# Scale before square: reordering the two readers of the heads' values, and the fourth head's transposes, in a fused GNN/FFN kernel

## The chip, the cores and the metric

The kernel runs on one core of a Trainium2 chip. The metric is the device time of one execution in microseconds (us). The core has a matmul engine (PE), a vector engine (DVE), a scalar engine (ACT), a GpSimd engine (POOL) and a sync engine (SP) that issues most transfers. Each works through its own list of instructions in order, and they meet through semaphores.

## What is computed

The reference is two layers on 625 nodes of 512 features: a hyperbolic graph convolution, a mixture of experts, a second graph convolution, and a grouped-query attention with a two-step output map. All the work around the change is in that last block. Cut to what matters, it is

```python
q  = (xn @ Wq_w + Wq_b)                    # 128 heads of 128
qk = einsum('bsghd,blgd->bghsl', q, kc) / sqrt(128)
z  = einsum('bghsl,blgd->bsghd', softmax(qk), vc)   # 625 x (128 heads * 128)
zn = z / max(norm(z), 1e-12) * sqrt(16384) * wz_g1
h1 = silu(zn @ wz_w1 + wz_b1)              # 625 x 1024
```

So of each head's values z two things are needed: z times the gain wz_g1, which goes into the product with wz_w1, and z squared, whose sum over all heads gives the norm that scales the product afterwards.

## The kernel before, in words

The 128 heads are taken in 32 blocks of HB = 4. The loop at lines 1239 to 1263 is a software pipeline over the blocks: in step i it starts the loads of block i+1 (`load`), runs the product of block i-2 with wz_w1 (`hidden`, line 1209: 98 small products, a fast matrix multiplication on quarters of the operands), transposes the attention of block i-1 for its heads 0 and 1 (`transposes`, line 1144), folds the query weights of block i into keys (`folded`, line 1103), turns the query weights of block i+1 on DVE (`turned`, lines 1097 to 1101), computes the values of the four heads of block i-1 (`value`, line 1155), builds the operand sums of block i-1 for its product (`prepared`, line 1195), and computes the scores of block i with their softmax (`scores`, line 1114).

Per head h the work around the change is this.

- `transposes(b, h)`: five PE transposes of the attention into a PSUM tile `atps` (line 1150) and two ACT copies into the SBUF tile `attT[h % 2]` (line 1153). There are two attT tiles, so heads 0 and 2 share one and heads 1 and 3 the other.
- `value(b, h)`: two products into a PSUM tile `zps` (line 1159), the square on ACT into `zs` (line 1162), the scaling on DVE into `zT` (line 1163), and the addition of `zs` into the running sum `zsq`, on POOL (line 1166) but for the last block, where it is on DVE (line 1168). The tile zs has one buffer (`bufs=1`, line 1161).

After the last block, `combined` (line 1266) is ordered behind the last addition to zsq (`combined(inner(0), valued)`, line 1281), and the norm is made from zsq in `scale_of_values` (line 1296).

What sets the order: the code's order is only a priority. The framework takes the program as a graph of instructions and lays down one list for each engine by a timed plan of its own; an instruction that stands earlier in the code but whose inputs are not there yet in that plan can be passed by a later one. The plan also hands out buffers (the PSUM pool of this part has four slots of two banks, shared by atps, zps, kbps, scps and h1ps) and puts the semaphore waits in. Two engines that read the same PSUM tile are kept apart, in the order of the code: in the kernel before, DVE's scaling waits for ACT's square of the same zps.

In the texts below v0 to v3 are the value products of heads 0 to 3 of a block, t2 and t3 the PE transposes of heads 2 and 3, copy 2 and copy 3 their ACT copies, and square 0, scaling 0, addition 0 and so on the three steps of line 1162, 1163 and 1166.

Of the kernel before, what the change touches and what calls it, by code (L numbers as in the profile page):

```python
# [22 lines left out]
OP = mybir.AluOpType  # L23
# [16 lines left out]
QN = 157  # L40
# [15 lines left out]
HB = 4  # L56
# [111 lines left out]
def layers_kernel(  # L168
# [10 lines left out]
    nc = tc.nc  # L179
    V, A, T = nc.vector, nc.scalar, nc.tensor  # L180
# [22 lines left out]
    b1T, bqT, g1T, gmT, bkT, bz1T, g2T = (cols[:, a:b] for a, b in (  # L203
        (0, 128), (128, 256), (256, 384), (384, 388), (388, 396), (396, 404), (404, 412)))
# [43 lines left out]
    def moments(behind=None, pieces=((0, NT),)):  # L248

        st = rpool.tile([P, NT, V.BN_STATS_DIM], F32, tag="ln_st", name="ln_st")  # L250
        mv = rpool.tile([P, NT, V.BN_AGGR_DIM], F32, tag="ln_mv", name="ln_mv")
        rs = R.new("ln_rs")
        for a, b in pieces:
            for t in range(a, b):
                read = V.bn_stats(st[:, t, :], x[:, t, :])
                if behind is not None:
                    order(read, behind)
                V.bn_aggr(mv[:, t, :], st[:, t, :])
            V.tensor_scalar(rs[:, a:b], mv[:, a:b, 1], LN_EPS, None, op0=OP.add)
            R.act(rs[:, a:b], rs[:, a:b], AF.Sqrt)  # L260
            R.inverse(rs[:, a:b], rs[:, a:b])
        return mv, rs, read
# [50 lines left out]
    with ExitStack() as es:  # L313
# [138 lines left out]
        def rotating(name):  # L452
            return big.tile([128, NT * D], F32, tag="rotating", name=name, bufs=2)
# [86 lines left out]
        def conv_out(raw, mapped, last):  # L540

            acc = [psum.tile([128, 512], F32, tag="ps", name="agps") for _ in range(NT)]
            if last:
                busy(acc[0], 18, mapped)
            for a, b in PIECES:
                for t in range(NT):
                    for i in range(a, b):
                        product = T.matmul(acc[t][:P], AT[:, i, tp(t)], raw[:, i, :], start=i == 0, stop=i == NT - 1)  # L548
            u = None if last else rotating("u")[:P].rearrange("p (t n) -> p t n", n=D)
            sq, s, inside = (RP[0, NT].new(name) for name in ("co_sq", "co_s", "co_in"))  # L550
            for a, b in PIECES:
                r = RP[a, b]
                for t in range(a, b):
                    junk = work.tile([P, D], F32, tag="junk", name="junk")
                    A.activation(junk, acc[t][:P], AF.Square, scale=dis[:, t : t + 1], accum_out=sq[:, t : t + 1])
                    if not last:
                        V.tensor_scalar(u[:, t, :], acc[t][:P], dis[:, t : t + 1], None, op0=OP.mult)
                s_p, in_p = r.expmap0(sq[:, a:b], "co")
                if last:
                    R.mul(s[:, a:b], s_p, dis[:, a:b])  # L560
                    for t in range(a, b):
                        V.scalar_tensor_tensor(x[:, t, :], acc[t][:P], s[:, t : t + 1], x[:, t, :],
                                               op0=OP.mult, op1=OP.add)
                else:
                    V.tensor_copy(s[:, a:b], s_p)
                    V.tensor_copy(inside[:, a:b], in_p)
            if last:
                product = busy(psum.tile([128, 512], F32, tag="ps", name="spare"), 31, product)
            return u, s, inside, product
# [6 lines left out]
        u = rotating("u")[:P].rearrange("p (t n) -> p t n", n=D)  # L576
# [13 lines left out]
        b_scale, _ = R2.in_ball(*b_norm, "b")  # L590
        s, inside = r.in_ball(*norm, "ex")
# [15 lines left out]
        for first in range(GROUP, EC, GROUP):  # L607
            last = min(first + GROUP, EC)
            group = counting(first, last)
            for j in range(first, last):  # L610
# [3 lines left out]
                if j == first + 8 and first == GROUP:  # L614
                    ps = psum.tile([128, 512], F32, tag="ps", name="colps")
# [4 lines left out]
                    ps = psum.tile([128, 512], F32, tag="ps", name="gtps")  # L620
# [8 lines left out]
        u, s, inside, _ = conv_out(sent, mapped, False)  # L629
# [3 lines left out]
    with ExitStack() as es:  # L633
# [42 lines left out]
        for a, b in PIECES:  # L676
            ps = psum.tile([128, 512], F32, tag="ps", name="lps")
# [40 lines left out]
        for g in range(G):  # L718
            ps = psum.tile([128, 512], F32, tag="ps", name="wkps")
# [17 lines left out]
        ps = psum.tile([128, 512], F32, tag="ps", name="bbps")  # L737
# [93 lines left out]
        def second_map(e):  # L831
            oe = work.tile([CAP, D], F32, tag="oe", name="oe")
            ps = psum.tile([128, 512], F32, tag="ps", name="ops")
            for hc in range(HC):
                T.matmul(ps[:CAP], hT[e][:, hc, :], w2[e][:, hc, :], start=hc == 0, stop=hc == HC - 1)  # L835
            return oe, V.tensor_tensor(oe, ps[:CAP], b2[e], op=OP.add)
# [34 lines left out]
        for e in range(NE):  # L871
# [4 lines left out]
            if e + 1 < NE:  # L876
                chosen(e + 1)
                oe, _ = second_map(e)
# [5 lines left out]
        for t in range(NT):  # L884
            ps = psum.tile([128, 512], F32, tag="ps", name="yps")
# [14 lines left out]
    with ExitStack() as es:  # L900
# [8 lines left out]
        for k in range(2):  # L909

            sT = big.tile([128, DC, N], F32, tag="sT", name="sT", bufs=2)
            for c in range(DC):
                for a, b in PIECES:
                    ps = psum.tile([128, 512], F32, tag="ps", name="stps")
# [7 lines left out]
            for t in range(NT):  # L922
                ps = psum.tile([128, 512], F32, tag="ps", name="l1ps")
# [16 lines left out]
    with ExitStack() as es:  # L940
# [11 lines left out]
        mv, rs, _ = moments()  # L952
# [14 lines left out]
        for a, b in PIECES:  # L967
            ps = psum.tile([128, 512], F32, tag="ps", name="hps")
# [4 lines left out]
        for a, b in PIECES:  # L973
            ps = psum.tile([128, 512], F32, tag="ps", name="wtps")
# [4 lines left out]
        ps = psum.tile([128, 512], F32, tag="ps", name="wsps")  # L979
# [18 lines left out]
        ps = psum.tile([128, 512], F32, tag="ps", name="wsps2")  # L998
# [7 lines left out]
        ps = psum.tile([128, 512], F32, tag="ps", name="xmps")  # L1006
# [6 lines left out]
        ps = psum.tile([128, 512], F32, tag="ps", name="swps")  # L1013
# [8 lines left out]
        for q in range(2):  # L1022
            ps = psum.tile([128, 512], F32, tag="ps", name="kcps")
# [5 lines left out]
            for i in range(4):  # L1029
                g = 4 * q + i  # L1030
                V.scalar_tensor_tensor(kcT[:, g, :], sums[:, :L], bkT[:, g : g + 1], ps[:, i * L : (i + 1) * L],
                                       op0=OP.mult, op1=OP.add)
        for q in range(2):
            ps = psum.tile([128, 512], F32, tag="ps", name="vcps")
# [8 lines left out]
        for q in range(2):  # L1043
            ps = psum.tile([128, 512], F32, tag="ps", name="qbps")
# [9 lines left out]
    with ExitStack() as es:  # L1054
# [5 lines left out]
        zsq = big.tile([128, 4 * QN], F32, name="zsq")  # L1060
# [4 lines left out]
        zT = big.tile([128, 7, 2, 2 * QN], F32, name="zT")  # L1065
# [5 lines left out]
        NB = G * H // HB  # L1071
# [6 lines left out]
        def banks(name):  # L1078
            return psum.tile([128, 2, 512], F32, tag="ps", name=name)
# [64 lines left out]
        def transposes(b, h):  # L1144
            ps = banks("atps")
            if b == h == 0:
                busy(ps[:, 0], 13, folded.last)
            for k, (p0, p1) in enumerate(PIECES):
                for t in range(p0, p1):
                    T.transpose(ps[:L, k, (t - p0) * P : (t - p0 + 1) * P], att[b][:, t, h * L : (h + 1) * L],  # L1150
                                ident[:P, :P])
            for k, (p0, p1) in enumerate(PIECES):
                A.activation(attT[h % 2][:, p0 * P : p1 * P], ps[:L, k, : (p1 - p0) * P], AF.Copy)  # L1153

        def value(b, h):
            g = b * HB // H
            ps = banks("zps")
            for u in range(2):
                T.matmul(ps[:, u, : 2 * QN], vc[:, g * DH : (g + 1) * DH], attT[h % 2][:, 2 * u * QN : 2 * (u + 1) * QN],  # L1159
                         start=True, stop=True)  # L1160
            zs = work.tile([128, 2, 2 * QN], F32, tag="zs", name="zs", bufs=1)
            A.activation(zs, ps[:, :, : 2 * QN], AF.Square)  # L1162
            scaled = V.tensor_scalar(zT[:, h % 2 : 4 : 2, h // 2, :], ps[:, :, : 2 * QN], g1T[:, b * HB + h : b * HB + h + 1],  # L1163
                                     None, op0=OP.mult)
            if b < NB - 1:
                nc.gpsimd.tensor_tensor(zsq, zsq, zs.rearrange("p u s -> p (u s)"), op=OP.add)  # L1166
                return scaled
            return V.tensor_tensor(zsq, zsq, zs.rearrange("p u s -> p (u s)"), op=OP.add)

        def zsums(z, to):  # L1170

# [67 lines left out]
        for i in range(NB + 1):  # L1239
            if i + 1 < NB:  # L1240
                load(i + 1)
            if i >= 2:
                hidden(i - 2)
            if i >= 2:

                transposes(i - 1, 0)
                transposes(i - 1, 1)
            if i < NB:
                folded(i)
            if i == 1:  # L1250
                transposes(0, 0)
                transposes(0, 1)
            if i + 1 < NB:
                turned(i + 1)
            if i >= 1:
                for h in range(HB):
                    valued = value(i - 1, h)
                    if h + 2 < HB:
                        transposes(i - 1, h + 2)
            if 1 <= i < NB:  # L1260
                prepared(i - 1)
            if i < NB:
                scores(i)
# [150 lines left out]
```

## Time and profile before

| what | value |
| --- | --- |
| median of 3 runs | 2293.77 us (2293.68 to 2294.13) |
| the profiled execution's own time | 2299.3 us |
| its span, first to last instruction | 2297.5 us |
| PE busy | 2230.4 us (97%) |
| DVE busy | 1618.5 us (70%) |
| POOL busy | 991.4 us (43%) |
| ACT busy | 814.8 us (35%) |
| mean granted PE clock | 0.989 |
| first square of heads' values (L1162) | at 630.5 us |
| last scaling of heads' values (L1163) | at 2195.3 us |

The profiled execution took 5.5 us more than the median run, 0.24%. The four-head blocks run from about 627 us to 2197 us, more than two thirds of the span, and they are nearly alike: where one block is shown, it stands for the others. A row of the timeline gives the start in us from the span's start, the length in us, the engine, the line, the operation, the tile written and those read, the number of instructions merged in the row, and in brackets how long the engine sat idle before it and on whom it waited. A row of the waits gives who waited on whom: us in total, times, the longest in us. A busy PE says little of itself, since the matmuls overlap and their ends are modelled; the distance from one row's start to the next is the better measure.

### The profile page before, as it was taken

The numbers are of one execution on the slowest core, as the hardware profiler recorded it, in microseconds if no ns is written. First come the engines' busy times: TensorE is split into PE (matmuls) and PEld (weight loads), VectorE is DVE, ScalarE is ACT, GpSimd is POOL, SyncE is SP. The second block draws the span as 40 slices with busy tenths as digits, with TensorE's granted clock in tenths as the row PEclk, the third lists the DMA queues.
The fourth block names the chain that finished last, engine by engine and source line by source line (L and its number), as shares of the span: only waits on it lengthen the run. The fifth ranks groups of instructions, "written<-read, shape, count | busy, mean of one in ns | idle before, by whom it ended". The sixth has DMA issues, their size and how long they took to land.

```text
span 2297.5 us, 34432 instructions
## 1 busy us (share of the span) xinstructions
PE 2230.4 (97%) x12812; PEld 1770.4 (77%) x12812; DVE 1618.5 (70%) x2303; ACT 814.8 (35%) x2773; POOL 991.4 (43%) x1063
## 2 busy tenths in 40 slices
PE   8999999999999999999999999999999999999987
PEld 5746777756788888888888888888888888888853
DVE  5845333233478888877888887788888778888782
ACT  2354111111333443344344334433443443344322
POOL 1000000100265566656556665555666555566531
PEclk8999999999999999999999999999999999999989
DMA  7002688771222222233222223322222332221110
GB/s 256 8 0 87 233 295 297 237 238 40 36 65 60 59 66 59 60 96 73 59 59 66 59 60 96 73 59 59 66 59 59 96 72 61 59 66 41 42 59 23
DMA packets 326025, 204.68 MB, mean 89 GB/s; under 512 B 275534, under 2 KB 279563, under 8 KB 321000
## 3 DMA queue, kind: packets, MB, share of 16 engines
q1 hardware_dynamic: 317371, 189.65, 28.0%
q10 hardware_dynamic: 3639, 7.56, 0.9%
q0 software_dynamic: 4848, 5.26, 0.9%
q8 instruction: 102, 1.67, 0.3%
q14 instruction: 65, 0.53, 0.1%
HBM read 197.18 MB, written 5.23 MB: 88 GB/s over the span
## 4 chain that ended last, share of the span: by engine, by line
PE 86%; DVE 4%; ACT 4%; POOL 2%; issue 2%; DMA 1%; ACTq 0%; POOLq 0%; DVEq 0%
PE h1ps L1222 35%; PE scps L1123 19%; PE kbps L1110 5%; PE hps L824 5%; PE ops L835 5%; PE zps L1159 3%; POOL zsq L1166 2%; ACT zs L1162 2%; PE stps L918 2%; PE eps L77 2%; PE agps L548 2%; PE atps L1150 2%; PE l1ps L925 1%; DMA b_row<-in_L_gnn_b_dram 1%; DVE hacc L1270 1%
## 5 line engine op out<-in xcount | busy, mean ns | idle before, releaser
L1234 DVE TENSOR_TENSOR hacc<-hacc,h1ps 128x942 f32<-128x942 f32 (+1 forms) x510 | 529.2, 1084 | 11.6 <-PE h1ps L1222 11.6
L1123 PE MATMUL scps<-keys,xnT 128*125 128x400 f32 x1280 | 435.1, 499 | 0.0
L1182 POOL TENSOR_TENSOR wq<-wz 128x256 f32<-128x256 f32 x248 | 241.0, 981 | 405.5 <-PE h1ps L1222 347.3
L1123 PEld LDWEIGHTS scps<-keys,xnT 128*125 128x125 f32 x1280 | 240.0, 188 | 185.1 <-issue 2.6
L1131 ACT ACTIVATE att<-att,a_top 125x100 f32<-125x100 f32 x640 | 231.9, 364 | 361.6 <-DVE a_top L1126 361.6
L1222 PE MATMUL h1ps<-zT,wq 128*128 128x157 f32 x1736 | 302.6, 296 | 0.0
L1222 PE MATMUL h1ps<-zq,wq 128*128 128x157 f32 x1736 | 302.5, 297 | 0.0
L1166 POOL TENSOR_TENSOR zsq<-zsq,zs 128x628 f32<-128x628 f32 x124 | 187.6, 1513 | 201.6 <-ACT zs L1162 201.6
L1222 PEld LDWEIGHTS h1ps<-zT,wq 128*128 128x128 f32 x1736 | 256.2, 189 | 0.0
L1222 PEld LDWEIGHTS h1ps<-zq,wq 128*128 128x128 f32 x1736 | 255.9, 190 | 0.0
L1153 ACT ACTIVATE attT<-atps 100x375 f32<-100x375 f32 (+1 forms) x256 | 92.4, 432 | 397.3 <-PE atps L1150 397.3
L1182 POOL TENSOR_TENSOR wq<-wz,wq 128x256 f32<-128x256 f32 x248 | 210.8, 850 | 19.5
L1163 DVE TENSOR_SCALAR zT<-zps,cols 128x628 f32<-128x628 f32 x128 | 111.6, 872 | 149.0 <-ACT zs L1162 147.6
L1142 ACT ACTIVATE att<-att,a_tot 125x100 f32<-125x100 f32 x620 | 170.2, 365 | 10.7 <-DVE a_tot L1132 10.7
L1159 PE MATMUL zps<-attT,vc 100*128 100x314 f32 x512 | 160.9, 436 | 10.6 <-ACT attT L1153 10.5
L1182 POOL TENSOR_TENSOR wq<-wsum,wq 128x256 f32<-128x256 f32 x186 | 161.5, 868 | 14.7 <-POOL wq L1182 0.3
L1182 POOL TENSOR_TENSOR wq<-wsum 128x256 f32<-128x256 f32 x186 | 135.8, 730 | 65.0 <-PE h1ps L1222 65.0
L1222 PE MATMUL h1ps<-zT,wz 128*128 128x157 f32 x992 | 152.6, 296 | 0.0
L1101 DVE STREAM_TRANSPOSE wqT<-wqraw 128x512 f32<-128x512 f32 x128 | 80.3, 681 | 101.1 <-PE kbps L1110 84.2
L1222 PEld LDWEIGHTS h1ps<-zT,wz 128*128 128x128 f32 x992 | 141.0, 189 | 9.1
L1162 ACT ACTIVATE zs<-zps 128x628 f32<-128x628 f32 x128 | 88.7, 693 | 125.0 <-POOL zsq L1166 111.3
L1159 PEld LDWEIGHTS zps<-attT,vc 100*128 100x128 f32 x512 | 87.4, 191 | 45.9 <-ACT attT L1153 26.9
(408 smaller groups left out, 3438.3 us busy)
## 6 DMA issues: line engine op xcount, KB each, us to landing
w<-in_L_ffn_w_dram SPq DMA_DIRECT2D x16, 4096.0 KB
wz<-in_L_ffn_wz_w_dram SPq DMA_DIRECT2D x32, 2048.0 KB
wqraw<-in_L_ffn_Wq_w_dram SPq DMA_DIRECT2D x512, 64.0 KB
cb<-qbias SPq DMA_DIRECT2D x32, 195.3 KB
wkv<-in_L_ffn_Wkv_w_dram SPq DMA_DIRECT2D x1, 4096.0 KB
W_raw<-in_L_gnn_W_dram SPq DMA_DIRECT2D x2, 1024.0 KB
w<-in_L_ffn_Wkv_w_dram SPq DMA_DIRECT2D x1, 2048.0 KB
l1w<-in_L_gnn_W_dram SPq DMA_DIRECT2D x2, 1024.0 KB
```

The costliest lines, as they stand in the source:

```text
L824: T.matmul(ps[:, i * CAP : (i + 1) * CAP], w1[e][:, c, hc * 128 : (hc + 1) * 128], xgT[e][:, c, :], start=c == 0, stop=c == DC - 1)
L835: T.matmul(ps[:CAP], hT[e][:, hc, :], w2[e][:, hc, :], start=hc == 0, stop=hc == HC - 1)
L1110: folded.last = T.matmul(ps[:, k, h * L : (h + 1) * L], wqT[b][h][:, (c + k) * 128 : (c + k + 1) * 128], kcT[:, b * HB // H, :], start=Tru ...
L1123: T.matmul(ps[:P, t - t0, : HB * L], xnT[:, c, tp(t)], keys[b][:, c, :], start=c == 0, stop=c == DC - 1)
L1131: A.activation(own, own, AF.Exp, bias=top[:, t, h : h + 1], accum_out=tot[:, t, h : h + 1])
L1142: A.activation(own, own, AF.Copy, scale=tot[:, t, h : h + 1])
L1159: T.matmul(ps[:, u, : 2 * QN], vc[:, g * DH : (g + 1) * DH], attT[h % 2][:, 2 * u * QN : 2 * (u + 1) * QN], start=True, stop=True)
L1162: A.activation(zs, ps[:, :, : 2 * QN], AF.Square)
L1166: nc.gpsimd.tensor_tensor(zsq, zsq, zs.rearrange("p u s -> p (u s)"), op=OP.add)
L1182: engine.tensor_tensor(to, x, y, op=OP.subtract)
L1222: T.matmul(ps[:, at % 6 // 3, at % 3 * QN : (at % 3 + 1) * QN], now[j][:, m * 128 : (m + 1) * 128], zquarter[b][j][:, place[i]], start=Tru ...
L1234: V.tensor_tensor(to, to, got, op=OP.add)
```

## The change

`value` is cut in two. What stays in it are the products and DVE's scaling, which now stands first among the readers of zps; ACT's square and the addition to zsq move into a new function `squared`, called afterwards. With that, the order of the two readers of zps turns over: ACT's square comes behind DVE's scaling. In the loop the transposes of head 2 stay behind the square of head 0, and the transposes of head 3, which stood behind the square of head 1, now stand ahead of it (and behind the scaling of head 1). The last block takes the same path, its additions on DVE as before. What `valued` means at the end is the same, the last addition to zsq.

```diff
@@ value @@
             for u in range(2):
                 T.matmul(ps[:, u, : 2 * QN], vc[:, g * DH : (g + 1) * DH], attT[h % 2][:, 2 * u * QN : 2 * (u + 1) * QN],
                          start=True, stop=True)
+            return ps, V.tensor_scalar(zT[:, h % 2 : 4 : 2, h // 2, :], ps[:, :, : 2 * QN],
+                                       g1T[:, b * HB + h : b * HB + h + 1], None, op0=OP.mult)
+
+        def squared(b, ps):
+
             zs = work.tile([128, 2, 2 * QN], F32, tag="zs", name="zs", bufs=1)
             A.activation(zs, ps[:, :, : 2 * QN], AF.Square)
-            scaled = V.tensor_scalar(zT[:, h % 2 : 4 : 2, h // 2, :], ps[:, :, : 2 * QN], g1T[:, b * HB + h : b * HB + h + 1],
-                                     None, op0=OP.mult)
-            if b < NB - 1:
-                nc.gpsimd.tensor_tensor(zsq, zsq, zs.rearrange("p u s -> p (u s)"), op=OP.add)
-                return scaled
-            return V.tensor_tensor(zsq, zsq, zs.rearrange("p u s -> p (u s)"), op=OP.add)
+            engine = nc.gpsimd if b < NB - 1 else V
+            return engine.tensor_tensor(zsq, zsq, zs.rearrange("p u s -> p (u s)"), op=OP.add)
@@ the loop over blocks @@
             if i >= 1:
                 for h in range(HB):
-                    valued = value(i - 1, h)
-                    if h + 2 < HB:
-                        transposes(i - 1, h + 2)
+                    ps, _ = value(i - 1, h)
+
+                    if h == 1:
+                        transposes(i - 1, 3)
+                    valued = squared(i - 1, ps)
+                    if h == 0:
+                        transposes(i - 1, 2)
```

No instruction is added or taken away, and no transfer is touched.

## The prediction, made before the result was known

> **What bounds the kernel now.** I read the page first: PE is busy 97% of the span, and the chain that ended last is 86% PE. So an edit on DVE, ACT and POOL can only matter where PE waits for them. I then took the waits of PE within the blocks, one block's timeline, and the last block's. PE's rows of one block, from the products of the values to the scores:
>
> ```profile
> 1083.69 1.23 PE L1159 MATMUL zps<-attT,vc 100*128 100x314 f32 x4
> 1084.76 0.70 PE L1150 MATMUL atps<-ident,att 125*100 125x125 f32 x5
> 1085.29 1.23 PE L1159 MATMUL zps<-attT,vc 100*128 100x314 f32 x4
> 1086.86 1.33 PE L1159 MATMUL zps<-attT,vc 100*128 100x314 f32 x4 [0.34 <-ACT attT L1153]
> 1088.02 13.60 PE L1123 MATMUL scps<-keys,xnT 128*125 128x400 f32 x40
> ```
>
> These are v1, t3, v2, v3 and the first scores. From start to start, v1 takes 1.07 us (1083.69 to 1084.76), v2 1.57 and v3 1.16. Free-running, v2 and v3 would take 1.07 each. The hole before v3 is thus 0.50 + 0.09 = 0.59 us (the page shows 0.34 of it idle, since matmul ends are modelled). It is PE's only one in the block: from 1088.18 to 1128.52 PE is busy throughout. The same wait stands in the list of waits 31 times, once for each block but the last.
>
> Why v3 is late, by ACT's rows of the same stretch:
>
> ```profile
> 1083.42 0.69 ACT L1162 ACTIVATE zs<-zps 128x628 f32<-128x628 f32 x1 [0.31 <-PE zps L1159]
> 1084.01 0.74 ACT L1153 ACTIVATE attT<-atps 100x375 f32<-100x375 f32 x2
> 1085.74 0.69 ACT L1162 ACTIVATE zs<-zps 128x628 f32<-128x628 f32 x1 [0.99 <-POOL zsq L1166]
> 1086.33 0.75 ACT L1153 ACTIVATE attT<-atps 100x375 f32<-100x375 f32 x2
> ```
>
> Square 1 waits for POOL's addition 0 to give zs back (1084.19, 1.52 us long), and copy 3, whose transposes had started at 1084.76, is queued behind it. v3 starts 0.53 us after copy 3 does.
>
> DVE's rows, same block:
>
> ```profile
> 1081.60 2.49 DVE L1101 STREAM_TRANSPOSE wqT<-wqraw 128x512 f32<-128x512 f32 x4 [2.85 <-PE kbps L1110]
> 1084.14 0.87 DVE L1163 TENSOR_SCALAR zT<-zps,cols 128x628 f32<-128x628 f32 x1
> 1086.47 0.87 DVE L1163 TENSOR_SCALAR zT<-zps,cols 128x628 f32<-128x628 f32 x1 [1.45 <-ACT zs L1162]
> ...
> 1092.00 1.32 DVE L1173 TENSOR_TENSOR zT<-zT 128x628 f32<-128x628 f32 x1
> 1093.36 0.81 DVE L1174 TENSOR_TENSOR zT<-zT 128x628 f32<-128x628 f32 x1
> ```
>
> Each scaling starts 0.04 us after its square ends, so the two readers of zps are kept apart. And the four weight transposes hold DVE until 1084.09, well after v0 could be read (1083.42).
>
> **The change, part by part, in that block's times.**
>
> *Scaling ahead of square.* Scaling 0 can't start before the weight transposes end: 1084.14 as now, to 1085.01. Square 0 becomes the waiting one: 1085.05 instead of 1083.42, 1.63 us later. Behind it on ACT are queued copies 2 and 3, and behind those v2 and v3; its addition on POOL comes later too. Everything depends on whether copy 2 is held up.
>
> *Copy 2.* In the code it stays behind square 0. But the lists are laid down by what is ready: in the last block ACT runs, against the code,
>
> ```profile
> 2189.07 0.48 ACT L1153 ACTIVATE attT<-atps 100x375 f32<-100x375 f32 x1 [0.80 <-PE atps L1150]
> 2189.45 0.69 ACT L1162 ACTIVATE zs<-zps 128x628 f32<-128x628 f32 x1
> 2190.02 0.38 ACT L1153 ACTIVATE attT<-atps 100x250 f32<-100x250 f32 x1
> ```
>
> the first part of copy 3 ahead of square 1, because zs wasn't free yet. DVE likewise passes L1175 by L1176, which does not need the operand just made. Here copy 2's inputs come from t2, which starts at 1083.16 right behind v0 and lasts some 0.5 us, while square 0 needs scaling 0, over a microsecond later. I take copy 2 ahead of square 0: about 1083.7 to 1084.5, so v2 starts at 1085.29 as now, cost nothing. If the plan keeps the code's order, see the first rival.
>
> *Copy 3.* Its two ACT instructions and five PE transposes move ahead of square 1 and no transfer goes with them; on PE the order v1, t3, v2, v3 is unchanged, on POOL nothing is passed but addition 1, which isn't needed by PE, and SP sees nothing. Copy 3 now follows square 0 instead of square 1. A copy starts 0.59 us after its square (1083.42 to 1084.01): 1085.05 + 0.59 = 1085.64. v3 can start 0.53 later, 1086.17, and is due behind v2 at 1085.29 + 1.07 = 1086.36. It fits by 0.19 us, so the hole closes: scores at 1086.36 + 1.07 = 1087.43 instead of 1088.02, **0.59 us a block, 18.3 us over 31**. The bounds of this term: nothing, if copy 3 slips by 0.8, and 0.59, since PE has no other hole here.
>
> *What is late next.* Squares 1 to 3 now wait for the additions. Square 0 ends at 1085.74, addition 0 at about 1087.3, square 1 runs 1087.4 to 1088.1, square 2 ends at 1090.4, square 3 at 1092.7. They give back PSUM slots: the second scores tile (due 1087.43 + 2.7 = 1090.1, eight products at 0.336) needs the slot of v1, the third (1092.8) that of v2, the product after them (1100.9) that of v3. The margins are 2.0, 2.4 and 8.2 us, so this costs nothing. POOL's next work now starts at 1103.84, 11.18 us after its additions.
>
> *DVE's sums beside POOL's additions.* Scalings 1 to 3 no longer wait for squares; the last ends near 1088.6 (v3 at 1086.36, readable 1.35 later as v0 is, plus 0.87) instead of 1091.97. So the eight sums of `prepared` start 3.4 us earlier, but three of the additions now lie beside them. The row: L1173 takes 1.32 us beside addition 3, L1174 of the same size 0.81 alone, so 0.5 each, 1.5 us in all. The Trainium skill ("SBUF — State Buffer", section "SBUF: two separate sides") speaks harder against the change: a GpSimd instruction and a VectorE instruction with two SBUF inputs lock their common port pair for a whole instruction, and the loser fully blocks. The trace agrees as far as it goes: L1173 began 0.65 us before the addition ended (1091.14 + 1.51) and finished 0.67 us after. By start-to-start times the sums need 4 x 0.73 + 4 x 1.21 and one added scores row 0.90, 8.7 us: done at 1097.3 without contention, 1098.8 by the row, and 1101.3 by the rule with about 4.0 us of additions served in full. PE reads the last sum at 1102.52 now, at 1101.93 afterwards. So it is covered even by the rule, by 0.6 us. I take nothing.
>
> *Last block.* DVE makes the additions here. Now each head costs the chain square (0.70), scaling (0.87), addition (0.73 to 1.00): from square 1 at 2189.45 to the last addition at 2196.89. Afterwards a scaling can run while ACT squares the head before. Scaling 0 from 2186.9 (no weight transposes here), square 0 to 2188.7 with copy 2 ahead of it, scaling 1, addition 0 to 2190.1, and then per head a square (0.75) and an addition (0.8) with the scalings in the gaps: the last addition at about 2194.9. `combined` hangs on it and everything behind on DVE. **2.0 us**; between 0.3 (if every addition is queued ahead of the next scaling) and 3.5 (DVE's own 4 x 0.87 + 4 x 0.75 without a gap).
>
> The sum is 18.3 + 2.0 = 20.3 us. Against the profiled execution: 2299.3 to 2279.0. Against the median, which is 0.24% below that execution: 2293.77 - 20.3 = **2273.5**.
>
> **The rivals.**
>
> *Square 0 stays ahead of copy 2 on ACT (slower).* For it: the code says so. Against: the last block's rows. Then copy 2 starts at 1085.64, v2 at 1086.17 instead of 1085.29, with its first weight load exposed (+0.09) v3 follows at 1087.33, scores at 1088.40: 0.38 later than now, 11.8 us over 31 blocks, less 2.0: 2303.6. It decides from the point where v2 is more than 0.5 us late, that is when scaling 0 ends after about 1084.6; it ends at 1085.01.
>
> *The hole closes by half.* The 0.19 us that copy 3 has to spare goes, or sums blocked by additions come up to 0.3 us too late for PE. For it: both margins are thin. 0.3 x 31 = 9.3 us saved: 2284.5.
>
> *PE gains nothing in the blocks.* Copy 3 still ends behind a zs wait, or what PE gains it waits out at the product. Against: L1222 shows no idle PE at all, and POOL waits for PE there (L1182, 0.70 us a time), not the reverse. Only the last block gains: 2291.8.
>
> **How the numbers follow.** A measurement of this kernel can tell about 0.2% (4.6 us) from no change. Chances: forecast 0.70, half 0.14, nothing 0.07, slower 0.09. Faster by over 0.2% is 0.70 + 0.14 = 0.84, the same 0.07, slower 0.09. The low end is the hole closed and the last block's best: 18.3 + 3.5 = 21.8, with a little for the hole's own error: 2270. The high end takes in the half: 2286. That leaves out 0.16.
>
> **What would show it.** In the profile after: no wait of PE's L1159 on ACT L1153 in the blocks, scores starting 2.14 us after v2, a block period of 49.7 us instead of 50.3; on ACT copy 2, square 0, copy 3, square 1 in that order; L1162 waiting for DVE L1163, no longer the reverse; the sums L1173 to L1176 longer but ending before PE asks; the last L1168 some 2 us sooner after the last block's transposes. The prediction is wrong if square 0 stands ahead of copy 2, if PE's L1222 shows a wait for DVE, or if v3 still waits.

## The result, and the profile after

| | before | changed |
| --- | --- | --- |
| median | 2293.95 us (4 runs, 2293.68 to 2295.53) | 2312.22 us (4 runs, 2310.83 to 2316.06) |
| ratio, 95% interval | | 1.0073 (1.0061 to 1.0085) |
| profiled execution, span | 2299.3, 2297.5 us | 2310.83, 2309.1 us |
| from the first v0 to the last block's v0 | 1556.4 us | 1574.9 us |
| from the last block's v0 to the end | 112.0 us | 109.9 us |
| period of a block | 50.32 us | 51.00 us |
| DVE busy | 1618.5 us | 1715.5 us |

The kernel became slower by 0.73%, where 0.89% faster was forecast. The profiled executions differ by 11.5 us only, because the code ahead of the first values, which the change does not touch, happened to take 4.9 us less in the later one. The loss is in the blocks: 18.5 us; from the last block's values on, 2.1 us come back. The period of a block is the time from its v0 to the next block's v0.

First the forecast's own place. PE's timeline of a block of the changed kernel (scaling is now L1161, the square L1167, POOL's addition L1169, DVE's operand sums for the product L1174 to L1177, and L1235 the additions to hacc, DVE's running sum of the product in SBUF, each of which empties a PSUM slot):

```profile
1083.59 1.23 PE L1159 MATMUL zps<-attT,vc 100*128 100x314 f32 x4
1084.65 0.70 PE L1150 MATMUL atps<-ident,att 125*100 125x125 f32 x5
1085.19 2.29 PE L1159 MATMUL zps<-attT,vc 100*128 100x314 f32 x8
1087.31 13.60 PE L1123 MATMUL scps<-keys,xnT 128*125 128x400 f32 x40
...
1110.77 0.77 PE L1223 MATMUL h1ps<-zT,wq 128*128 128x157 f32 x4 [0.26 <-DVE hacc L1235]
...
1128.28 0.74 PE L1150 MATMUL atps<-ident,att 125*100 125x125 f32 x5 [0.20 <-DVE hacc L1235]
1129.33 1.92 PE L1110 MATMUL kbps<-kcT,wqT 128*128 128x100 f32 x15 [0.31 <-DVE hacc L1235]
```

v2 and v3 now run in one piece; from v2 to the scores it is 2.12 us, 2.73 before. The hole is closed. But there are three new ones, all waits for DVE's additions to hacc: PE needs a PSUM slot that DVE has not emptied. By starts they are 1110.77 instead of 1110.34, 1128.28 instead of 1127.91 and 1129.33 instead of 1128.81: 0.43 + 0.37 + 0.52 = 1.32 us. The block gained 0.61 and lost 1.3. The list of waits has each of the three 29 times: the first and the last of the 31 periods (49.77 and 46.19 us, before 50.40 and 46.79) gained 0.6 and lost nothing.

Why DVE is late, by its own timeline in the same block:

```profile
1088.42 1.69 DVE L1174 TENSOR_TENSOR zT<-zT 128x628 f32<-128x628 f32 x1
1090.14 0.81 DVE L1175 TENSOR_TENSOR zT<-zT 128x628 f32<-128x628 f32 x1
1090.88 2.12 DVE L1177 TENSOR_TENSOR zT<-zT 128x628 f32<-128x628 f32 x1
...
1093.76 2.50 DVE L1174 TENSOR_TENSOR zq<-zT 128x1099 f32<-128x1099 f32 x1
...
1099.93 0.99 DVE L1124 TENSOR_TENSOR att<-scps,cb 125x800 f32<-125x800 f32 x1
...
1104.86 2.17 DVE L1235 TENSOR_TENSOR hacc<-hacc,h1ps 128x942 f32<-128x942 f32 x2
1109.35 0.28 DVE L1132 RECIPROCAL a_tot<-a_tot 125x20 f32<-125x20 f32 x1 [2.32 <-ACT att L1131]
1109.55 6.30 DVE L1235 TENSOR_TENSOR hacc<-hacc,h1ps 128x942 f32<-128x942 f32 x6
```

and POOL's:

```profile
1090.25 2.08 POOL L1169 TENSOR_TENSOR zsq<-zsq,zs 128x628 f32<-128x628 f32 x1 [0.81 <-ACT zs L1167]
1093.13 1.96 POOL L1169 TENSOR_TENSOR zsq<-zsq,zs 128x628 f32<-128x628 f32 x1 [0.81 <-ACT zs L1167]
```

Two things are to be read. The sums start 3.6 us earlier than before, yet three of them are longer: L1177 takes 2.12 us where the same size took 0.81. It starts at 1090.88 while addition 2 runs (1090.25 to 1092.33) and ends 0.67 us after it; addition 2 itself, 1.51 us alone, had been held up 0.6 us by the sum before. So most of the head start is used up. And DVE, behind its six rows of the scores (L1124 and L1126), meets the reciprocal L1132 after *two* additions to hacc, and stands 2.32 us until ACT's last exponential is done. In the kernel before it met it after *three*:

```profile
1105.31 3.22 DVE L1234 TENSOR_TENSOR hacc<-hacc,h1ps 128x942 f32<-128x942 f32 x3
1109.79 0.28 DVE L1132 RECIPROCAL a_tot<-a_tot 125x20 f32<-125x20 f32 x1 [1.26 <-ACT att L1131]
1109.98 4.21 DVE L1234 TENSOR_TENSOR hacc<-hacc,h1ps 128x942 f32<-128x942 f32 x4
1114.46 1.14 DVE L1234 TENSOR_TENSOR hacc<-hacc,h1ps 128x942 f32<-128x942 f32 x1 [0.27 <-PE h1ps L1222]
```

The diff has nothing about L1132. I take it that its place moved because in the framework's timed plan the scalings, and with them DVE's list, come sooner, so that the exponentials are done sooner there; no run here shows the plan itself. Measured from the start of the scores, DVE goes on to its additions 21.96 us later before (1088.02 to 1109.98) and 22.24 after (1087.31 to 1109.55), with one addition more (1.05) still to make: 0.28 + 1.05 = 1.33 us, about PE's loss. The bracket in the last row before, 0.27, is nearly all the slack that DVE had, the time by which it could be later without holding up PE. The first of the weight sums that follow (L1183, which makes the product's weight operands; 1.65 us in the mean of the blocks instead of 1.33, beside POOL's L1183) takes about as much away again. The two periods without a loss fit: in the first the reciprocal still stands behind the third piece of the product, and in the last, where it stands behind the second and waits 2.31 us, DVE goes on already 21.62 us after the start of the scores and has no weight sums behind it.

### The profile page after: what moved, and what is told of

The parts are those of the page before. It is cut to its first block, busy times and chain, and to the rows that moved or that the text cites. A ratio compares the mean times of both kernels' runs of the same rounds, so it can differ in the third digit from the quotient of the medians.

```text
span 2309.1 us, 34430 instructions
## 1 busy us (share of the span) xinstructions
PE 2231.7 (97%) x12812; PEld 1769.5 (77%) x12812; DVE 1715.5 (74%) x2303; ACT 822.0 (36%) x2773; POOL 1026.6 (44%) x1063
## 4 chain that ended last, share of the span: by engine, by line
PE 56%; DVE 27%; ACT 11%; issue 4%; DMA 1%; POOLq 0%; ACTq 0%; DVEq 0%; SPq 0%; POOL 0%
PE h1ps L1223 21%; ACT att L1131 10%; PE zps L1159 6%; PE hps L824 5%; PE kbps L1110 5%; PE ops L835 5%; DVE hacc L1235 4%; DVE zq L1174 3%; DVE zT L1177 3%; PE atps L1150 2%; DVE zT L1174 2%; PE stps L918 2%; PE agps L548 2%; DVE zq L1175 2%; DVE zq L1176 2%
## 5 line engine op out<-in xcount | busy, mean ns | idle before, releaser
L1235 DVE TENSOR_TENSOR hacc<-hacc,h1ps 128x942 f32<-128x942 f32 (+1 forms) x510 | 526.4, 1084 | 3.4 <-PE h1ps L1223 3.3
L1183 POOL TENSOR_TENSOR wq<-wz 128x256 f32<-128x256 f32 x248 | 240.9, 981 | 307.5 <-PE h1ps L1223 251.1
L1169 POOL TENSOR_TENSOR zsq<-zsq,zs 128x628 f32<-128x628 f32 x124 | 219.0, 1766 | 267.8 <-ACT zs L1167 267.8
L1183 POOL TENSOR_TENSOR wq<-wz,wq 128x256 f32<-128x256 f32 x248 | 214.2, 864 | 19.5
L1183 POOL TENSOR_TENSOR wq<-wsum,wq 128x256 f32<-128x256 f32 x186 | 161.3, 867 | 22.9 <-PE h1ps L1223 10.5
L1183 POOL TENSOR_TENSOR wq<-wsum 128x256 f32<-128x256 f32 x186 | 135.5, 729 | 71.3 <-PE h1ps L1223 71.3
L1159 PE MATMUL zps<-attT,vc 100*128 100x314 f32 x512 | 152.5, 430 | 0.1
L1167 ACT ACTIVATE zs<-zps 128x628 f32<-128x628 f32 x128 | 88.7, 693 | 155.8 <-POOL zsq L1169 146.6
L1161 DVE TENSOR_SCALAR zT<-zps,cols 128x628 f32<-128x628 f32 x128 | 110.3, 862 | 41.2 <-PE zps L1159 37.9
L1110 PE MATMUL kbps<-kcT,wqT 128*128 128x100 f32 x1024 | 122.0, 277 | 8.8 <-DVE hacc L1235 8.8
```

The source lines that it names most:

```text
L1110: folded.last = T.matmul(ps[:, k, h * L : (h + 1) * L], wqT[b][h][:, (c + k) * 128 : (c + k + 1) * 128], kcT[:, b * HB // H, :], start=Tru ...
L1169: return engine.tensor_tensor(zsq, zsq, zs.rearrange("p u s -> p (u s)"), op=OP.add)
L1183: engine.tensor_tensor(to, x, y, op=OP.subtract)
L1235: V.tensor_tensor(to, to, got, op=OP.add)
```

## The experiments

My theory after the result (A): the reciprocal, taken too early in DVE's list, holds back the additions to hacc and with them PSUM. Rivals: (B) POOL's additions, which lock DVE's sums out, are the cause; (C) DVE sets the pace as soon as PE's hole closes, so that there was nothing to gain. Ratios are to the kernel before, run beside them.

| run | ratio (95%) | median us | block us |
| --- | --- | --- | --- |
| changed | 1.0073 (1.0061 to 1.0085) | 2312.22 | 51.00 |
| e1 only the transposes moved | 1.0004 (0.9994 to 1.0013) | 2295.5 | 50.32 |
| e2 changed, reciprocal behind the third addition | 0.9917 (0.9901 to 0.9934) | 2275.99 | 49.71 |
| e3 changed, POOL writes and does not read | 0.9921 (0.9904 to 0.9937) | 2277.55 | 49.70 |
| e4 before, copy 3 forced ahead of square 1 | 1.0064 (1.0047 to 1.0080) | 2308.2 | 50.66 |
| e5 changed, reciprocal behind the first addition | 1.0164 (1.0147 to 1.0181) | 2334.53 | 51.74 |
| e6 changed, two zs buffers | 0.9942 (0.9925 to 0.9958) | 2282.56 | 49.84 |
| e7 before, two zs buffers | 0.9908 (0.9892 to 0.9925) | 2275.32 | 49.70 |
| e8 before, reciprocal behind the fourth addition | 0.9995 (0.9986 to 1.0005) | 2295.25 | 50.32 |
| e9 changed, two zs buffers, reciprocal behind the fourth | 0.9909 (0.9892 to 0.9925) | 2275.32 | 49.70 |

**e1: one half of the change.** This edit and those below are cut to what matters; the remarks in them are mine.

```diff
-                    valued = value(i - 1, h)          # square, scaling, addition
-                    if h + 2 < HB:
-                        transposes(i - 1, h + 2)
+                    ps = value(i - 1, h)              # products only
+                    if h == 1:
+                        transposes(i - 1, 3)
+                    valued = read(i - 1, h, ps)       # square, scaling, addition
+                    if h == 0:
+                        transposes(i - 1, 2)
```

> One half of the change alone: the transposes of head 3 stand ahead of the square of head 1 in the code, the square stays ahead of the scaling. If the order of the code alone moved copy 3, v3's hole of 0.59 us a block would close (2276). The lists say otherwise: apart from two ACT rows of the last block they are those of the kernel before, so I expect 2294, no change, and the whole effect of the change to come from the turned-over readers. If the moved transposes were what cost time, 2312.

No difference, and the block is 50.32 us. Moving the transposes in the code moves nothing in the lists of the blocks: square 1 stays ahead of copy 3. I take it that copy 3 passed square 1 in the changed kernel because the *square* became late behind its scaling. The other half alone was not run, so whether the moved transposes are needed at all is not shown.

**e2: the reciprocal put back.**

```diff
-            V.reciprocal(tot, tot)                    # in scores
+            order(V.reciprocal(tot, tot), added)      # in hidden, added = third addition to hacc
```

> The changed kernel with only DVE's reciprocal of the softmax sums (L1132) put back to where the kernel before has it, behind the third addition to hacc of the block instead of the second; all else as changed. Theory A (the reciprocal, taken too early, holds DVE 2.3 us for the last exponential, and the PSUM slots of the product come back late): DVE's wait falls to about 1.3 us, PE's three stalls of 1.31 us a block shrink to 0.3 or less, about 31 us saved, 2281. Theory B (POOL's additions, which lock DVE's sums out, are the cause, wherever the reciprocal stands): 2308 to 2312. Theory C (PE's hole was no gain at all because DVE sets the pace once it closes): 2295 or more.

In the code the ACT copies that use the reciprocal move with it. By the two traces, though, nothing differs in the lists of PE, ACT and POOL, and on DVE's only the reciprocal's place. DVE's timeline of e2 (the reciprocal is L1144 here, the additions to hacc L1241, the sum that was L1177 is L1183):

```profile
1081.80 2.12 DVE L1183 TENSOR_TENSOR zT<-zT 128x628 f32<-128x628 f32 x1
...
1095.78 3.22 DVE L1241 TENSOR_TENSOR hacc<-hacc,h1ps 128x942 f32<-128x942 f32 x3
1100.27 0.28 DVE L1144 RECIPROCAL a_tot<-a_tot 125x20 f32<-125x20 f32 x1 [1.28 <-ACT att L1131]
1100.47 5.34 DVE L1241 TENSOR_TENSOR hacc<-hacc,h1ps 128x942 f32<-128x942 f32 x5
```

One instruction moved by one place takes 36 us off the changed kernel. The sums are as long as in it (1.69, 2.12 and 2.50 us), so B as stated falls: the lock-out (a DVE sum and a POOL addition going one after the other) with the reciprocal in its old place costs PE nothing. C falls too, since PE keeps the whole hole: 49.71. It came out better than expected (2281), as no stall remained.

**e3: the lock-out taken away.** The kernel leaves out the squares of blocks 0 to 30 from the norm.

```diff
-            return engine.tensor_tensor(zsq, zsq, zs.rearrange("p u s -> p (u s)"), op=OP.add)
+            if b < NB - 1:
+                return nc.gpsimd.memset(zs, 0.0)
```

> The changed kernel with POOL's addition to zsq in blocks 0 to 30 replaced by a POOL instruction that only writes zs over (the norm then lacks those heads), all lists otherwise the same. If POOL shuts DVE out only by reading, the four sums that took 0.4 to 1.3 us longer return to 0.8 and 1.3, DVE is some 2.9 us earlier, the exponentials end before the reciprocal is reached, and PE's stalls vanish: theories A and B both give 2275, C gives 2295 or more. If it shuts DVE out by writing too, the sums stay longer by what the writes last, and the time lies between.

DVE's timeline of e3:

```profile
1081.69 0.81 DVE L1175 TENSOR_TENSOR zT<-zT 128x628 f32<-128x628 f32 x1
1082.53 0.81 DVE L1176 TENSOR_TENSOR zT<-zT 128x628 f32<-128x628 f32 x1
...
1099.22 0.28 DVE L1132 RECIPROCAL a_tot<-a_tot 125x20 f32<-125x20 f32 x1 [0.67 <-ACT att L1131]
```

and POOL's:

```profile
1081.66 0.62 POOL L1169 MEMSET zs<- 128x628 f32 x1 [0.78 <-ACT zs L1167]
```

The first sum runs 0.81 us with a POOL write on top of it. With the sums short, DVE is early, and the reciprocal behind the *second* addition waits 0.67 instead of 2.32: no stall on PE. POOL's instruction is also shorter, 0.62 us for 1.51, and gives zs back sooner; but in these blocks neither PE nor DVE waits for the squares, here or in the changed kernel. So the loss needs both, the lock-out and the early reciprocal: e2 has the first alone, e3 the second alone, and neither costs PE anything. The reciprocal's place does no harm where the sums run as fast as they do here.

**e4: the hole closed in another way.**

```diff
             square = A.activation(zs, ps[:, :, : 2 * QN], AF.Square)
+            if h == 1:
+                order(square, copied)                 # copied = the last part of copy 3
```

> The kernel before with only ACT's copy 3 forced ahead of square 1; the square stays ahead of the scaling, so DVE's scalings and sums come 0.36 us later than before and POOL's additions mostly do not lie beside the sums. v3's hole closes. Theory C: PE gains nothing, 2294. Theory A: the reciprocal stands behind the third addition as before and waits 1.3 us or a little more; part of the gain stays, 2278 to 2288.

I expected a gain and it is slower. PE's timeline of e4:

```profile
1101.90 0.80 PE L1228 MATMUL h1ps<-zq,wz 128*128 128x157 f32 x4 [0.69 <-DVE zq L1181]
```

and DVE's:

```profile
1097.23 0.98 DVE L1126 TENSOR_REDUCE a_top<-att 125x8 f32<-125x800 f32 x1
...
1100.55 1.30 DVE L1181 TENSOR_TENSOR zq<-zT,zq 128x1099 f32<-128x1099 f32 x1
```

The scalings still follow their squares, the second 0.45 us later than before when counted from v0. And the plan put two scores rows among the sums where it had one, L1124: L1126 has come to it, 0.90 us from its start to the next. The last sum ends at 1101.85, and PE, earlier by the hole, is due to read it at 1101.04 and waits. By the period this wait costs 0.96 and the closed hole brings 0.61. The added row is as long as PE is late, 0.86 us, so the run does not show that the scalings must come ahead of the squares, or end earlier, for the hole to be of use. It shows once more a row that moved though the edit does not name it; the two delays were not tried apart.

**e5: the reciprocal one place earlier still.** The edit is that of e2 with the first addition in place of the third, and the second addition ordered behind the reciprocal.

> The changed kernel with the reciprocal L1132 forced one addition earlier still: behind the first addition to hacc of the block and ahead of the second; DVE's list is otherwise the same. Theory A: one more addition (1.04 us) now waits behind the last exponential, DVE's wait grows from 2.3 to about 3.4 us and PE loses about 1 us more a block: 2312 + 31 = 2343. If the reciprocal's place were only a companion of something else, 2312.

DVE's wait is 3.36 us, as expected, and the time goes the expected way, by less: 0.91% or 21 us instead of 31, 0.74 us a block. PE's timeline shows one stall in place of three:

```profile
1117.35 0.80 PE L1231 MATMUL h1ps<-zT,wz 128*128 128x157 f32 x4 [1.76 <-DVE hacc L1243]
```

It is long enough that DVE has caught up by the block's end, where the changed kernel stalled twice more.

**e6: less lock-out, reciprocal's place untouched.**

```diff
-            zs = work.tile([128, 2, 2 * QN], F32, tag="zs", name="zs", bufs=1)
+            zs = work.tile([128, 2, 2 * QN], F32, tag="zs", name="zs", bufs=2)
```

> The changed kernel with two buffers for zs instead of one; every engine's list is the same, only the wait of a square for the last addition but one instead of the last. Squares and additions come sooner, the four additions end near 1092 instead of 1095 in the block's times, and less of them lies beside DVE's sums: 2.4 us instead of 4.1. If the lock-out of the sums is what makes the exponentials late (A and B together), DVE's wait at the reciprocal falls from 2.3 to about 1 us and PE loses 0.2 us a block instead of 1.31: 2278 to 2284. If the lock matters little, 2305 or more.

The time is in the expected range, but not by the expected way:

```profile
1091.88 0.98 DVE L1124 TENSOR_TENSOR att<-scps,cb 125x800 f32<-125x800 f32 x1
...
1101.28 0.28 DVE L1132 RECIPROCAL a_tot<-a_tot 125x20 f32<-125x20 f32 x1 [2.31 <-ACT att L1131]
1101.48 6.30 DVE L1235 TENSOR_TENSOR hacc<-hacc,h1ps 128x942 f32<-128x942 f32 x6
```

The wait at the reciprocal did not shrink. Between the last sum and L1132 DVE runs six scores rows and two additions without a gap, and ACT's exponentials start behind the second of those rows, so the wait is the same whenever that run begins. What moved is the run itself: the sums are 0.70 us shorter together, and the first scores row starts 11.92 us after the scores on PE (1079.96 to 1091.88) instead of 12.62. With that DVE goes on to its additions 21.52 us after the scores' start instead of 22.24, and the weight sum behind them is back at 1.22 us; of PE's 1.3 us 0.13 are left in most blocks (three of the 31 periods took 0.77 more, and three waits for DVE's hacc stand in PE's list).

**e7: the same edit on the kernel before.**

> The kernel before with two buffers for zs; the lists are the same but for two ACT rows of the last block, so the reciprocal stays behind the third addition and the square stays ahead of the scaling. Square 1 no longer waits for addition 0, copy 3 starts near 1085.5 instead of 1086.33, and v3's hole closes; the scalings follow their squares and end near 1089.5. Theory A: the sums start early enough for PE and the reciprocal is not reached too soon, so the block takes 49.7 us: 2275 to 2279. If only scaling first lets the hole be used, as the run with copy 3 forced forward suggests, 2290 or more.

49.70, the gain that the change was forecast to bring, from one number, with the square still ahead of the scaling and the lists of the blocks as they were. In DVE's timeline of e7 the reciprocal, behind three additions, waits 0.72 us:

```profile
1097.74 1.14 DVE L1234 TENSOR_TENSOR hacc<-hacc,h1ps 128x942 f32<-128x942 f32 x1 [0.46 <-PE h1ps L1222]
1099.59 0.28 DVE L1132 RECIPROCAL a_tot<-a_tot 125x20 f32<-125x20 f32 x1 [0.72 <-ACT att L1131]
```

and DVE waits for PE again, so it has slack. The scalings end earlier here too, since square 1 no longer waits for addition 0.

**e8: a control.** The edit of e2, on the kernel before, with the fourth addition.

> The kernel before with only the reciprocal L1132 moved from behind the third to behind the fourth addition to hacc. A control: in the kernel before PE waits nowhere for DVE, only for copy 3, so DVE's wait of 1.27 us goes but PE gains nothing: 2294. If the place of the reciprocal is worth time by itself, 2285 or less.

No change, as expected: the place of the reciprocal is worth nothing while PE waits only for copy 3.

**e9: both together.** The edits of e6 and e2 (fourth addition) on the changed kernel.

> The changed kernel with two buffers for zs and the reciprocal L1132 behind the fourth addition to hacc. With the reciprocal alone or the second buffer alone a block already takes 49.70 to 49.84 us, and PE has no hole left in it, so the blocks can give nothing more than 49.70; the last block keeps the 2 us that scaling first saves there. Theory A with B: 2273 to 2276, within 0.1% of the kernel before with two buffers (2275). If another hole opened, or the last block gave something more, it would lie outside that.

2275.32 us, the same as e7. Four kernels at 49.70 or 49.71 and none lower, and PE waits nowhere in these blocks: with these products that is PE's own time for a block.

## Why the prediction was wrong, point by point

- *Copy 2 ahead of square 0, copy 3 behind square 0*: right. ACT's rows are copy 2 at 1083.85, square 0 at 1084.84, copy 3 at 1085.45 and square 1 at 1087.15, and v3 waits for nothing. The 0.59 us were there, 0.61 by the difference of 50.32 and 49.71 in e2. By e1 the moved transposes of head 3, to which the forecast gave this, do nothing by themselves.
- *The last block*: right. The last addition ends 9.55 us after the block's v0 instead of 11.38, so 1.8 us sooner where 2.0 were forecast; the other 0.3 of the table's 2.1 come behind it and belong to no term.
- *PSUM slots of the values*: right, no PE wait for them.
- *DVE's sums beside POOL's additions*: the size was within its bounds, and nearer to the rule of the Trainium skill ("SBUF — State Buffer", section "SBUF: two separate sides") than to the 0.5 us a piece of the row: three sums took 0.88, 1.31 and 1.20 us more than the 0.81 and 1.30 of the same sizes alone, 3.4 us in all for 1.5 by the row and 4.0 by the rule. The last sum ended at 1100.02. The 1098.8 and 1101.3 that were given count a scores row among the sums, which now runs behind them; with it the end is 1100.92, nearer to the rule again. PE did not wait for it.
- **The step that failed** is the end of that same point: "So it is covered even by the rule, by 0.6 us. I take nothing." I asked only whether PE gets the last sum in time. Behind the sums on DVE are queued the six scores rows, on which the exponentials hang, then the reciprocal, which waits for the exponentials, and behind it the additions that empty PSUM for PE. That run has hardly any slack, 0.27 us, and I never looked: "L1222 shows no idle PE at all" was read as distance from trouble, which it is not. With that, I took DVE's list to stay as it was while I argued at length that ACT's would not. The missing term was 1.3 us of waiting a block. It is made up of 1.05 for the addition that changed sides with the reciprocal and 0.28 for the lateness; the slack of 0.27 takes off about what the longer weight sum, 0.32, adds. With the 29 periods that lost it, 31 x 0.61 - 29 x 1.3 is about -19 us, where the blocks measured -18.5 and the forecast had +18.3.
- *The rivals*: none was this. The half-closed hole named sums blocked by additions, but at PE's reading of the sums, and with a gain left (its 2284.5 also leaves out the last block's 2.0 us, which the other two rivals count). The slower rival, square 0 ahead of copy 2, did not occur. The one sentence that did catch it is among the signs of error: PE's L1222 showing a wait for DVE.

What stays open: whether the place of L1124, which went from among the sums to behind them, has a share of its own in the 0.28 us. L1126 starts 1.02 us after L1124 where it stands right behind it (1099.93 to 1100.95), and a row behind L1124 among the sums starts 0.90 after it (1096.87 to 1097.77 before). So I estimate that share at 0.12 us; it was not tried alone. Open too are whether the moved transposes are needed, and why the plan chose the place of the reciprocal.

## What to carry to other kernels

When an edit makes one engine earlier, follow what is queued behind the moved work on that engine until it reaches the engine that sets the pace, and measure the slack in that run by its idle brackets; no idle time on the other side says nothing of how near it is. Where a framework plans each engine's list, an edit can move instructions that the diff does not name: compare the lists of all engines, and look for the one that waits for another engine ahead of work that returns buffers. A buffer more (e7) removes a wait without turning over an order that something else leans on.

## What the hardware showed

An addition on POOL and a DVE sum with two SBUF inputs went one after the other, in both directions (DVE 0.81 to 2.12 us, POOL 1.51 to 2.08). The later of the two ended behind the earlier by its own length alone, less about 0.14 us (L1177 0.67 us behind addition 2, for 0.81 alone), while a POOL instruction that only writes, 0.62 us for the same tile, lay on top of a sum without making it longer. The forecast had counted DVE's side of it, not POOL's. It also means that the length of a sum depends on what POOL happens to do: the same lists cost PE nothing without the lock-out (e3) and 1.3 us a block with it.
